# Last recurrence of a four-layer network: more routed tiles per state in the first two halves, ends of halves twice as fast, experts without delay, the gate in its half

## Chip, cores and metric

One core of a Trainium2 chip runs the whole network in one launch. The metric is the device time of one execution in microseconds (us). The engines run on their own lists of instructions, each in its order, and wait for each other by semaphores: PE (TensorE, matmul; PEld loads its weights), DVE (VectorE), ACT (ScalarE), POOL (GpSimd) and SP (SyncE, which issues most transfers; POOL issues gathers and accumulating transfers). PSUM is the memory that matmuls write, in eight banks.

## The reference, cut to what matters

A batch of 4 sequences of 1024 rows and 128 features goes through four layers, each an "attention" and a feed-forward part with a layer norm behind the sum. The change lies in the third layer's feed-forward part (routed experts) and the fourth layer, `x` being float32 throughout:

```python
def _L2_ffn_ref(x, router_w, w13, w2):       # 8 experts, the best two a row
    probs = jax.nn.softmax(jnp.einsum('bsh,eh->bse', x, router_w), axis=-1)
    weights, indices = jax.lax.top_k(probs, 2)
    ...

def _L3_attn_ref(resid, ...):                # E = 256 channels, N = 16 states
    x = resid * lax.rsqrt(jnp.mean(resid * resid, -1, keepdims=True) + EPS) * norm_w
    skip = x @ skip_w.T
    xe = x @ in_w.T
    ...                                      # causal convolution of 4, silu -> xs
    delta = jax.nn.softplus(xs @ wd1.T @ wd2.T + wd2_b)
    A = -jnp.exp(A_log)
    Bm = xs @ wb.T
    Cm = xs @ wc.T
    def step(h, inp):
        d_l, b_l, c_l, x_l = inp
        h = jnp.exp(d_l[:, :, None] * A) * h + (d_l * x_l)[:, :, None] * b_l[:, None, :]
        y_l = jnp.einsum('ben,bn->be', h, c_l)
        return (h, y_l)
    ...
    y = (y + xs * W_D) * jax.nn.silu(skip)
    return resid + y @ out_w.T

def _L3_ffn_ref(x, Wr, br, W1, b1, W2, b2):  # 8 experts, all computed, gated by top-p
    ...
    h = jax.nn.relu(jnp.einsum('bth,ehf->betf', x, W1) + b1[None, :, None, :])
    y = jnp.einsum('betf,efh->beth', h, W2) + b2[None, :, None, :]
    return jnp.einsum('bte,beth->bth', gate, y)
```

## The kernel before

The kernel is written with generators: a part of the work is a Python generator that issues instructions and yields, and a driver calls `next` on several of them by turns. A library puts the instructions of this stage into an order for each engine from what it reckons to be ready, so a list's order follows the driver's turns but isn't the same. Buffers come from pools that turn round in the order of issue; a tile waits until the one it takes the place of has been read.

The fourth layer works on eight halves of sequences (`halves` in `l3`, 512 rows each; half 0 and 1 are of the first sequence). For each half there are four pieces of work:

- `l3_prepare`: norm, convolution, `xs`; then `pdb` on PE (line 1784 copies it on ACT, line 1785 writes the rows `Bm` and `Cm` to DRAM, from where SP reads them back on all partitions as `bn` and `cn`), and `pd` on PE, from which ACT and DVE make `dl` (delta) and, in line 1809, `ud` (delta times `xs`).
- `l3_scan`: the recurrence, one state of 16 at a time for all 512 rows. POOL makes `db = ud * bn` (line 1845), ACT `da = exp(dl * A)` (1849), DVE scans (1850), POOL makes `hc = db * cn` (1861). From half 2 on (`b > 0`) POOL joins the `hc` of two states by an accumulating transfer (line 1865); PE sums `hc`, or the joined pairs, into two banks with an identity matrix (`pys`). Halves 0 and 1 thus have 16 sums and the others 8, the eighth with states 14 and 15.
- `l3_sum`: the last sums, and `xs * W_D + pys` on DVE (line 1882); `l3_finish`: the gate (`psk` on PE, tanh on ACT, two products on DVE), the output projection (`po`), the norm, and the router of the experts (`prl`, then a chain on DVE that ends with `gt`). Then the half goes to the list `todo`.
- `l3_experts`: the eight experts of each half in `todo`, one half after the other: `pgt` and `pb2` first, then for each expert four `ph` (128x512) with a ReLU on ACT (line 1973), sixteen `py` (128x128) and four accumulating steps on DVE (1989); weights `wh` are loaded by SP two experts ahead. On PE every float32 matmul shows as two records in the trace.

`moe` is the third layer's routed part, still running: per tile (23 a sequence, 92 in all) SP loads the expert's weights `wx`, PE does four `ph` and two `py`, and after a sequence's last tile POOL gathers 16 blocks of rows (line 1529) for its combination. Its tiles of the last sequence can't begin before that sequence's rows have been scattered, by `m2["rest"]`, one step a state.

The driver is the loop over `l3_scan(u)` in `l3`: after each state of half `i` it takes one step of the end of the half before (`end`, `l3_sum` and `l3_finish`), one of the next half's preparation (`nxt`), one of `moe` (two in half 0), and three of the experts, or four once `moe` has ended. A half in `todo` ages by one a state, and its experts start when it is older than 3. All of these matmuls but `pys` take their banks from four that go by the tag `ff`. What is left at a half's end of `end` and `nxt` is issued there, and before halves 1, 3 and 5 as much of `moe` as the half behind them needs.

Of the kernel before, what the change touches and what calls it, by code (L numbers as in the profile page):

```python
# [10 lines left out]
F32 = mybir.dt.float32  # L11
I32 = mybir.dt.int32
U32 = mybir.dt.uint32
AF = mybir.ActivationFunctionType
ALU = mybir.AluOpType
# [3 lines left out]
P = 128  # L19
# [21 lines left out]
E3, NST, DDELTA, KCONV = 256, 16, 64, 4  # L41
# [17 lines left out]
class Net:  # L59
# [1535 lines left out]
    def l3(self, moe, fp):  # L1595

        c3 = self.c3  # L1600
        halves = [dict(b=b, h=h) for b in range(B) for h in range(2)]
        for i, u in enumerate(halves):
            u["prev"] = halves[i - 1] if u["h"] else None
        halves[0] = dict(self.c3["first"], **{k: halves[0][k] for k in ("prev",)})
        for i, u in enumerate(halves[1:], 1):
            u["prev"] = halves[i - 1] if u["h"] else None
        work = self.l3_experts(fp)
        end = iter(())
        for i, u in enumerate(halves):
            nxt = iter(())  # L1610
            if i + 1 < len(halves):
                if halves[i + 1]["h"] == 0:
                    while "done" not in self.m2["st"][halves[i + 1]["b"]]:
                        next(moe)
                nxt = self.l3_prepare(halves[i + 1])
            for f in self.l3_scan(u):
                next(end, None)
                next(nxt, None)
                for k in range(1):
                    next(self.m2["rest"], None)  # L1620
                busy = next(moe, moe) is not moe
                if i == 0:
                    for k in range(1):
                        next(moe, None)
                for k in range(3 if busy else 4):
                    next(work)
                for v in c3["todo"]:
                    v["age"] += 1
            for f in chain(end, nxt):
                pass  # L1630
            end = chain(self.l3_sum(u), self.l3_finish(u))
        for f in end:
            next(work)
        c3["all"] = True
        for f in work:
            pass

    def l3_experts(self, fp):


        c3 = self.c3
        heads, self.wh = [], {}

        def others():

            while len(heads) < 2 and c3["todo"] and ("all" in c3 or c3["todo"][0]["age"] > 3):
                heads.append((c3["todo"].pop(0), []))
            return heads[1:]

        i = 0  # L1650
        while True:
            others()
            if "all" in c3 and c3["banks"]:

                c3["banks"].close()
                c3["banks"] = None
                c3["ctx"].enter_context(self.banks(ff=8))
            if heads:
                u = heads[0]
                if not u[1]:  # L1660
                    yield from self.l3_ffn_head(*u, fp)
                yield from self.l3_ffn(*u, i, fp, others)
                heads.pop(0)
                i += NE
            elif "all" in c3:
                return
            else:
                yield
# [146 lines left out]
    def l3_scan(self, u):  # L1815


        nc, c3, b, h = self.nc, self.c3, u["b"], u["h"]
        sp, wp, aneg = c3["sp"], c3["wp"], c3["aneg"]
        wout = c3["we"][:, :, ND:]  # L1820
        xnT, xs, dl, ud, rows = (u[k] for k in ("xnT", "xs", "dl", "ud", "rows"))
        carry = wp.tile([P, 2, NST], F32, name="carry") if h == 0 else u["prev"]["carry"]
        u["carry"] = carry
        u["py"] = py = []
        u["sums"] = sums = []

        def add(n, hc):
            if not py:
                py.extend(self.psb(f"y{ec}", [P, 512], f"pys{ec}") for ec in range(2))
                u["first"] = n  # L1830
            for ec in range(2):
                self.mm(py[ec], self.ident, hc[:, ec, :], n == u["first"], n == NST - 1)

        u["add"] = add
        for n in range(NST):
            bc = []
            for i, nm in enumerate(("bn", "cn")):
                t = wp.tile([P, 1, 512], F32, name=nm, bufs=4)
                r = i * NST + n
                nc.sync.dma_start(  # L1840
                    out=t[:, 0, :], in_=rows[r : r + 1, :].to_broadcast([P, 512])
                )
                bc.append(t.to_broadcast([P, 2, 512]))
            db = wp.tile([P, 2, 512], F32, name="db", bufs=4)
            nc.gpsimd.tensor_mul(db, ud, bc[0])  # L1845
            for ec in range(2):
                j = ec * NST + n
                da = self.psb("da", [P, 512], "da")
                nc.scalar.activation(da, dl[:, ec, :], AF.Exp, scale=aneg[:, j : j + 1])  # L1849
                nc.vector.tensor_tensor_scan(  # L1850
                    db[:, ec, :],
                    da,
                    db[:, ec, :],
                    carry[:, ec, n : n + 1] if h else 0.0,
                    ALU.mult,
                    ALU.add,
                )
            if h == 0:
                nc.scalar.copy(carry[:, :, n : n + 1], db[:, :, 511:512])
            hc = wp.tile([P, 2, 512], F32, name="hc", bufs=4)  # L1860
            nc.gpsimd.tensor_mul(hc, db, bc[1])  # L1861
            if n % 2 and b > 0:

                hc0 = sums.pop()[1]
                nc.gpsimd.dma_start(out=hc0, in_=hc, accum_op=ALU.add)
                sums.append((n, hc0, n + 2))
            else:
                sums.append((n, hc, n + 2))
            for k in range(2):
                if sums and sums[0][2] <= n:  # L1870
                    add(*sums.pop(0)[0:2])
            yield

    def l3_sum(self, u):

        while u["sums"]:
            u["add"](*u["sums"].pop(0)[0:2])
            if u["sums"]:
                yield
        for ec in range(2):  # L1880
            x = u["xs"][:, ec, :]
            self.nc.vector.scalar_tensor_tensor(
                x, x, self.col("W_D", i=ec), u["py"][ec], ALU.mult, ALU.add
            )

    def l3_finish(self, u):


        nc, c3, b, h = self.nc, self.c3, u["b"], u["h"]
        sp, wp = c3["sp"], c3["wp"]  # L1890
        ff = lambda s, n: self.psb("ff", s, n)
        wout = c3["we"][:, :, ND:]
        yt = u["xs"]
        for ec in range(2):
            p = ff([P, 512], "psk")
            self.mm(p, c3["wskip"][:, 0, ec * P : (ec + 1) * P], u["xnT"])

            t = sp.tile([P, 512], F32, name="th")
            nc.scalar.activation(t, p, AF.Tanh, scale=0.5)
            nc.vector.scalar_tensor_tensor(p, t, 1.0, p, ALU.add, ALU.mult)  # L1900
            nc.vector.scalar_tensor_tensor(
                yt[:, ec, :], yt[:, ec, :], 0.5, p, ALU.mult, ALU.mult
            )
            yield
        po = ff([P, 4, D], "po")
        for k in range(4):
            for ec in range(2):
                self.mm(
                    po[:, k, :],
                    yt[:, ec, k * P : (k + 1) * P],  # L1910
                    wout[:, ec, :],
                    ec == 0,
                    ec == 1,
                )

        r = sp.tile([P, 4, D], F32, name="ss_r", tag="s2")
        nc.vector.scalar_tensor_tensor(
            r, self.xN[b][:, 4 * h : 4 * h + 4, :], 2.0, po, ALU.mult, ALU.add
        )
        yield  # L1920
        yield from self.norm_parts(wp, r, b, 4 * h, 4, ps=ff, act=True, slow=True)
        yield
        n = NC // 2
        pr, g, rank, pj, cum = self.router(sp, b, c3["wr"], c3["br"], ps=ff, c0=4 * h, n=n)
        q, cum = cum
        nc.vector.tensor_mul(g, q, pj)
        nc.vector.reduce_sum(cum, g, AX.X)

        nc.vector.tensor_single_scalar(cum, cum, TOP_P, ALU.is_lt)
        nc.vector.scalar_tensor_tensor(cum, rank, 1.0, cum, ALU.is_le, ALU.max)  # L1930
        u["gt"] = sp.tile([P, n, NE], F32, name="gt", bufs=8)
        nc.vector.tensor_mul(u["gt"], pr, cum)
        u["age"] = 0
        c3["todo"].append(u)
# [268 lines left out]
```

## Time and profile before

| what | us |
| --- | --- |
| median of 3 runs (lowest, highest) | 2328.13 (2327.18, 2331.37) |
| profiled execution | 2329.42 |
| its span, first to last instruction | 2327.6 |
| PE busy in the span | 1994.8 (86%) |
| DVE | 1348.4 (58%) |
| ACT | 1205.4 (52%) |
| POOL | 1024.8 (44%) |

The span is what the views of the profile divide; 1.8 us of the profiled execution lie around it. Up to about 1400 us the first three layers run, and the eight halves of the recurrence lie between 1407 and 2177 us, by POOL's `hc` products; behind them come the experts that are left. A share of busy time over the whole span says little about either stage, so the stages have to be read one by one. In rows of the view of time, the columns are start, duration, engine, line, operation, out<-in, shape, count, and in brackets how long the engine had been idle and what ended that; a PE row's line is that of the helper that issues all matmuls (127), so that a tile's name tells which it is.

### The profile page before, as it was taken

The page shows a single profiled execution, that of the slowest core. Times are in us where ns is not written, and L with a number is a line of the kernel's source. Part 1 is how long each engine was busy: PE and PEld are TensorE (multiplying, and loading weights), DVE is VectorE, ACT ScalarE, POOL GpSimd, SP SyncE. Part 2 cuts the span into 40 slices and gives each one's busy share as a digit, 9 for nine tenths or more (in the row PEclk, how much of TensorE's full clock was granted, in tenths as well). Part 3 has the DMA queues.
Part 4 walks back from the last instruction along what each step waited for, and adds up shares of the span by engine and source line. Part 5 has one row for each costly group of instructions (what it writes and reads, how often), then busy time and mean ns, then how long its engine had stood idle before and what let it go on. Part 6 is the DMA issues. An engine that isn't in the chain of part 4 may idle for free. (4 is left out here: it accounts for less than half of the span.)

```text
span 2327.6 us, 46367 instructions
## 1 busy us (share of the span) xinstructions
PE 1994.8 (86%) x17802; PEld 1395.0 (60%) x17802; DVE 1348.4 (58%) x3693; ACT 1205.4 (52%) x2617; POOL 1024.8 (44%) x813
## 2 busy tenths in 40 slices
PE   6667979979999999999979857678898989889888
PEld 3455655544477777787767654355655556546556
DVE  7458743433445554654655557767776767776421
ACT  6543433332244444454565556566668766666343
POOL 5000230000123244234143259989887887769300
PEclk9757979979999999999999978889999989899899
DMA  3000110014000010031222176457765666666421
GB/s 105 0 19 18 31 38 6 14 40 140 1 3 2 3 37 22 25 88 42 84 77 72 49 221 182 146 165 204 219 175 162 180 173 163 180 164 177 100 59 50
DMA packets 138701, 211.62 MB, mean 91 GB/s; under 512 B 18613, under 2 KB 75952, under 8 KB 138096
## 3 DMA queue, kind: packets, MB, share of 16 engines
q1 hardware_dynamic: 126192, 173.87, 24.7%
q0 software_dynamic: 12288, 34.79, 7.2%
q8 instruction: 140, 2.29, 0.4%
q14 instruction: 81, 0.66, 0.1%
HBM read 160.29 MB, written 23.16 MB: 79 GB/s over the span
## 5 line engine op out<-in xcount | busy, mean ns | idle before, releaser
L1059 POOL TENSOR_TENSOR qt<-r_q,sb_c_turn 128x256 f32<-128x256 f32 (+1 forms) x256 | 164.4, 663 | 446.7 <-ACT r_q L1051 441.0
L1861 POOL TENSOR_TENSOR hc<-db,cn 128x1024 f32<-128x1024 f32 x128 | 311.3, 2453 | 64.4 <-PE pys L127 20.4
L1845 POOL TENSOR_TENSOR db<-ud,bn 128x1024 f32<-128x1024 f32 x112 | 283.7, 2597 | 30.6 <-DVE pmv L159 19.1
L127 PEld LDWEIGHTS py<-wh,hh 128*128 128x128 f32 x2048 | 251.8, 196 | 67.8 <-issue 38.7
L127 PE MATMUL ph<-xT,wh 128*128 128x512 f32 x512 | 262.5, 634 | 21.7 <-ACT hh L1973 8.0
L127 PE MATMUL py<-wh,hh 128*128 128x128 f32 x2048 | 257.2, 280 | 13.0 <-ACT hh L1973 10.1
L1973 ACT ACTIVATE hh<-ph,sb_cols 128x512 f32<-128x512 f32 x256 | 170.6, 682 | 146.2 <-PE ph L127 119.9
L1117 DVE TENSOR_TENSOR a<-pa_m,sb_c_near 128x256 f32<-128x256 f32 x256 | 96.6, 419 | 204.2 <-PE pa_m L127 204.2
L1074 ACT ACTIVATE kN<-kp_mo,sb_c_trig 128x128 f32<-128x128 f32 x448 | 130.2, 372 | 131.9 <-PE kp_mo L131 122.1
L1849 ACT ACTIVATE da<-dl,aneg 128x512 f32<-128x512 f32 x224 | 153.2, 689 | 84.1 <-DVE db L1850 83.3
L127 PE MATMUL pys<-hc,sb_c_ident 128*128 128x512 f32 x320 | 162.0, 636 | 24.6 <-POOL hc L1861 15.0
L1850 DVE TENSOR_TENSOR_SCAN db<-da,carry,db 128x512 f32<-128x512 f32 x128 | 156.8, 1266 | 25.9 <-ACT da L1849 12.5
L127 PEld LDWEIGHTS ph<-xT,wh 128*128 128x128 f32 x512 | 93.5, 202 | 115.0 <-issue 65.7
L1850 DVE TENSOR_TENSOR_SCAN db<-da,db 128x512 f32<-128x512 f32 x128 | 149.1, 1205 | 14.3 <-ACT da L1849 8.2
L1989 DVE SCALAR_TENSOR_TENSOR h_acc<-py,gt,h_acc 128x128 f32<-128x128 f32 x256 | 71.9, 342 | 140.4 <-PE py L127 140.4
L127 PE MATMUL pqk<-xT,wE 128*128 128x256 f32 x512 | 137.7, 393 | 8.2 <-ACT coT L1193 4.2
L127 PEld LDWEIGHTS pys<-hc,sb_c_ident 128*128 128x128 f32 x320 | 61.7, 206 | 90.0 <-issue 59.1
L127 PEld LDWEIGHTS pqk<-xT,wE 128*128 128x128 f32 x512 | 89.4, 195 | 22.1 <-DVE cv L1036 8.1
L729 POOL DMA_INDIRECT orows<-o,ix x20 | 18.9, 946 | 185.3 <-DVE o L727 158.8
L131 PE MATMUL pt<-sb_c_ident,xN 128*128 128x128 f32 x224 | 54.5, 345 | 52.1 <-ACT xN L174 33.9
L1193 ACT COPY coT<-pt 128x512 f32<-128x512 f32 x64 | 37.6, 587 | 114.7 <-PE pt L131 114.7
L127 PE MATMUL po<-ht,wD 128*128 128x512 f32 x192 | 93.7, 595 | 0.0
(457 smaller groups left out, 4342.4 us busy)
## 6 DMA issues: line engine op xcount, KB each, us to landing
wx<-in_wF SPq DMA_DIRECT2D x92, 384.0 KB, 3.4
bn<-rows SPq DMA_DIRECT2D x128, 256.0 KB, 4.9
cn<-rows SPq DMA_DIRECT2D x128, 256.0 KB, 4.5
wh<-in_wH SPq DMA_DIRECT2D x64, 512.0 KB, 3.9
hc<-hc POOLq DMA_DIRECT2D x48, 512.0 KB, 7.1
xrows<-zero SPq DMA_DIRECT2D x4, 1472.0 KB, 12.4
xg<-xrows SPq DMA_DIRECT2D x20, 256.0 KB, 3.1
yrows<-ys SPq DMA_DIRECT2D x20, 256.0 KB, 3.3
```

The lines of the kernel that those rows point to most:

```text
L127: return self.nc.tensor.matmul(out=out, lhsT=lhsT, rhs=rhs, start=start, stop=stop)
L131: self.nc.tensor.transpose(out, in_, self.ident[0:n, 0:n])
L1059: nc.gpsimd.tensor_mul(u["qt"][:, m, a:], u["q"][:, a:], c2["turn"][:, m, o + a : o + 2 * P])
L1074: self.nc.scalar.activation(u["kN"][:, c, m, :], pk[:, c, :], AF.Copy, scale=trig[:, k, m : m + 1])
L1117: nc.vector.tensor_mul(u["a"][:, i, :, :], pa[i], self.c2["near"][:, None, :].to_broadcast([P, 2, P]),)
L1193: nc.scalar.copy(oT, pt)
L1845: nc.gpsimd.tensor_mul(db, ud, bc[0])
L1849: nc.scalar.activation(da, dl[:, ec, :], AF.Exp, scale=aneg[:, j : j + 1])
L1850: nc.vector.tensor_tensor_scan(db[:, ec, :], da, db[:, ec, :], carry[:, ec, n : n + 1] if h else 0.0, ALU.mult, ALU.add,)
L1861: nc.gpsimd.tensor_mul(hc, db, bc[1])
L1973: nc.scalar.activation(ht, ph, AF.Relu, bias=self.col("h_b1", i=e * NK + k))
L1989: nc.vector.scalar_tensor_tensor(acc[:, c, :], py[:, c, :], gt[:, c, e : e + 1], acc[:, c, :], ALU.mult, ALU.add,)
```

## The change

It issues the same kinds of instructions in other turns:

- per state, `end` takes two steps and not one; `moe` takes four in half 0 (two before), two in half 1 (one before) and one in the others as before; the experts take three in the last half in any case;
- a half's experts may start once it is older than 0, not 3;
- the gate moves out of `l3_finish` (where it took two steps) into `l3_gate`, called inside `l3_scan` at states 9 and 12 of the same half, with a tile for each of the two channel blocks; `l3_sum` multiplies by it;
- in the last half the last two states aren't joined by a transfer, so that it has nine sums.

```diff
+            u["final"] = final = i + 1 == len(halves)
             for f in self.l3_scan(u):
-                next(end, None)
+                for k in range(2):
+                    next(end, None)
                 next(nxt, None)
...
                 busy = next(moe, moe) is not moe
-                if i == 0:
-                    for k in range(1):
-                        next(moe, None)
-                for k in range(3 if busy else 4):
+                for k in range((3, 1)[i] if i < 2 else 0):
+                    next(moe, None)
+                for k in range(3 if busy or final else 4):
                     next(work)
...
-            while len(heads) < 2 and c3["todo"] and ("all" in c3 or c3["todo"][0]["age"] > 3):
+            while len(heads) < 2 and c3["todo"] and ("all" in c3 or c3["todo"][0]["age"] > 0):
...
             nc.gpsimd.tensor_mul(hc, db, bc[1])
-            if n % 2 and b > 0:
-
+            if n in (9, 12):
+                self.l3_gate(u, n // 12)
+            if n % 2 and b > 0 and not (u["final"] and n == NST - 1):
                 hc0 = sums.pop()[1]
                 nc.gpsimd.dma_start(out=hc0, in_=hc, accum_op=ALU.add)
...
         for ec in range(2):
-            x = u["xs"][:, ec, :]
+            x, p = u["xs"][:, ec, :], u["py"][ec]
             self.nc.vector.scalar_tensor_tensor(
-                x, x, self.col("W_D", i=ec), u["py"][ec], ALU.mult, ALU.add
+                p, x, self.col("W_D", i=ec), p, ALU.mult, ALU.add
+            )
+            self.nc.vector.scalar_tensor_tensor(
+                x, u["gate"][ec], 0.5, p, ALU.mult, ALU.mult
             )
+
+    def l3_gate(self, u, ec):
+
+        nc, c3 = self.nc, self.c3
+        p = self.psb("ff", [P, 512], "psk")
+        self.mm(p, c3["wskip"][:, 0, ec * P : (ec + 1) * P], u["xnT"])
+        t = c3["sp"].tile([P, 512], F32, name=f"th{ec}")
+        nc.scalar.activation(t, p, AF.Tanh, scale=0.5)
+        nc.vector.scalar_tensor_tensor(t, t, 1.0, p, ALU.add, ALU.mult)
+        u.setdefault("gate", []).append(t)
...
-        for ec in range(2):
-            p = ff([P, 512], "psk")
-            self.mm(p, c3["wskip"][:, 0, ec * P : (ec + 1) * P], u["xnT"])
-
-            t = sp.tile([P, 512], F32, name="th")
-            nc.scalar.activation(t, p, AF.Tanh, scale=0.5)
-            nc.vector.scalar_tensor_tensor(p, t, 1.0, p, ALU.add, ALU.mult)
-            nc.vector.scalar_tensor_tensor(
-                yt[:, ec, :], yt[:, ec, :], 0.5, p, ALU.mult, ALU.mult
-            )
-            yield
```

## The prediction

> **What bounds the kernel now.** I read the page first, then busy time by stretches cut at the ends of the halves, then POOL's waits, then the order of time on PE, POOL and DVE at one change of halves. Below, each stretch but the first and the last runs from the end of a half's last `hc` product (state 15; I call that moment T) to the next half's T. Columns: us, then busy PE, PEld, DVE, ACT, POOL, the granted PE clock, DMA.
>
> ```profile
> 1407.10:1471.90 64.80, 46.58 (x139) 23.34 (x140) 42.07 (x60) 38.48 (x79) 64.80 (x29) 0.83 0.52 160
> 1471.90:1579.10 107.20, 80.10 (x364) 52.49 (x363) 78.42 (x140) 67.43 (x136) 91.81 (x50) 0.90 0.55 163
> 1579.10:1670.40 91.30, 76.48 (x394) 52.29 (x394) 71.85 (x139) 63.83 (x136) 79.82 (x39) 0.96 0.73 205
> 1670.40:1791.00 120.60, 105.86 (x535) 70.00 (x534) 85.26 (x164) 85.90 (x155) 100.52 (x59) 0.96 0.66 179
> 1791.00:1879.10 88.10, 79.79 (x357) 49.08 (x356) 67.46 (x136) 64.42 (x125) 75.72 (x38) 0.94 0.67 178
> 1879.10:1968.70 89.60, 85.46 (x424) 56.47 (x423) 62.80 (x108) 58.64 (x97) 81.47 (x42) 0.96 0.64 171
> 1968.70:2076.80 108.10, 97.20 (x465) 62.72 (x464) 76.44 (x151) 75.82 (x132) 81.97 (x42) 0.94 0.67 179
> 2076.80:2176.60 99.80, 84.27 (x402) 54.20 (x401) 68.23 (x136) 59.21 (x92) 81.31 (x41) 0.91 0.62 167
> 2176.60:2327.60 151.00, 134.13 (x703) 94.08 (x701) 34.24 (x120) 58.09 (x93) 0.88 (x1) 0.92 0.19 55
> ```
>
> Half 0 is POOL's alone (64.80 of 64.80). In halves 2 to 7 POOL has 76 to 82 us of work a half (100.5 with the 16 gathers of half 3) and PE nearly as much; the length of a half is POOL's work plus its waits. After the last T only PE works, on experts. POOL's waits from half 2 on (total, times, longest):
>
> ```profile
> POOL hc L1861 <- PE pys L127: 20.4, 11, 5.2
> POOL db L1845 <- DVE pmv L159: 19.1, 1, 19.1
> POOL db L1845 <- issue: 11.5, 1, 11.5
> POOL yg L1529 <- ACT xN L174: 7.6, 1, 7.6
> ```
>
> The second and third are single waits at changes of halves (5 to 6, 6 to 7): the next half's first `db` needs `ud`, the end of `l3_prepare`. At the other changes POOL goes on within 0.5 to 2.1 us. The change 6 to 7, POOL and PE in order of time (start, us):
>
> ```profile
> 2077.14 0.88 POOL L1865 DMA_DIRECT2D hc<-hc  x1 [0.30 <-DVE h_acc L1989]
> 2089.52 9.25 POOL L1845 TENSOR_TENSOR db<-ud,bn 128x1024 f32<-128x1024 f32 x4 [11.51 <-issue]
> ```
> ```profile
> 2070.73 1.96 PE L127 MATMUL pd<-db,sb_s_d 65*128 65x512 f32 x4
> 2072.53 3.74 PE L127 MATMUL py<-wh,hh 128*128 128x128 f32 x32
> 2076.11 3.60 PE L127 MATMUL pys<-hc,sb_c_ident 128*128 128x512 f32 x8
> 2085.92 3.78 PE L127 MATMUL pys<-hc,sb_c_ident 128*128 128x512 f32 x4 [6.21 <-DMA hc<-hc]
> ```
>
> What to see: PE goes through its list in its order. The half's last `pys` can't run before the accumulating DMA of the last pair has landed, 9.1 us after T (2076.81 to 2085.92), and all behind it waits. Here `pd` (what `ud` is made of) stands ahead of that `pys`; so `ud` lags only because DVE has L1882, which needs that `pys`, in front of the second `ud`.
>
> **The change, part by part.** I take the order in which the built programs' instructions stand on each engine, and price it with rows of before. H6.8 is the eighth (last) `pys` pair of half 6.
>
> *Ends twice as fast, experts at once.* In the changed order experts of half h-1 start at H.4 to H.6 of half h, before at H.7 or behind the half. Behind the last `pys` of all stand 224 `py` and 52 `ph` of experts, before 256 and 60: two experts fewer. One expert is 3.44 (`ph`) + 3.57 (`py`) us in the chain that ended last, so 14.0 us leave the tail. Price of the move: the experts' matmuls now stand in front of the next half's `pdb` and `pd`. In before, `pd` stands two or more pairs ahead of the last `pys` at every change (ahead of H6.6, H5.7, H4.5). In the changed order:
> - 5 to 6 and 6 to 7: H.8, 16 `py`, 2 `ph`, then `pd`. So T + 9.1 (DMA) + 2.1 (`pys`, 2085.92 to 2088.01) + 3.6 + 1.7 + 2.0 (`pd`) = T+18.5 for `pd`.
> - 4 to 5: `pd` is behind H4.7, `pdb` and an expert's 16 `py` and 2 `ph`. POOL issues that pair's DMA two `hc` (2.45 each) and 0.9 before T; it lands at T+3.0; + 2.1 + 1.9 + 5.3 + 2.0 = T+14.3.
> - 3 to 4: second `pd` behind H3.6, 13 `py`; its DMA is issued at T-11.8 (three `hc`, a `db`, two issues), lands T-3.0; + 2.1 + 1.0 + 2.9 + 1.0 = T+4.0.
> - 2 to 3: H2.8, then 16 `py`, a `ph`, `pdb`, 3 `ph` (these hide ACT's 0.7 for L1784), `pd`: T + 9.1 + 2.1 + 4.4 + 1.9 + 2.6 + 2.0 = T+22.1.
>
> From `pd` to the second `ud`: 13.3, 16.3, 14.4, 14.1, 16.0, 13.5 us in before, and 11.7 (2072.7 to 2084.4) had L1882 not stood between. While POOL stalls, ACT and DVE have no scans, so I take 12; ends 11.7 and 16.3. First `db`: T+30.5 twice, T+26.3, T+16, T+34.1. Before: T+20.8, +12.7, +0.6, +2.1, +0.5. Differences 9.7, 17.8, 25.7, 13.9, 33.6. In the last, 8 of the 16 gathers (L1529, 1.25 us apart) now lie in the stall, 10 us, and the 7.6 us wait ahead of them goes: 16.0 left. Sum **+83**. Behind the waiting H.8 on PE are the experts and `pd`; on DVE the new L1884, and behind it `h_acc` and `dl`; on POOL `db`, thus the whole next half. The 87 us from a half's first `db` to its T (1989.5 to 2076.8, 2089.5 to 2176.6) remain. PE can't refill POOL's lost time: its work between two last `pys` is 75 to 100 us, less than the periods of 103 to 118 us that result.
>
> In exchange PE comes to each half less late. Of the in-half waits of POOL, 20.4 (`pys`), 3.0 (`hc` DMA) could go, 23 us at most, 0 at least; I take half, **-12**.
>
> *Last half:* the last pair isn't joined by a DMA: one `pys` pair (1.7 us) more on PE, one issue (0.9) less on POOL, and no 9.1 us after T. But the pair before, issued 3.4 us before T, still stands ahead: it lands at T+5.4, and + 2.1 + 0.9 + 3.4 puts the last `pys` at T+11.8 (before T+14.2). Then the changed order has no expert between the router's `prl` and `pgt`, which took 10.6 us in half 7 of before (2165.6 to 2176.2): about 10 us of idle PE. Tail: 2.4 earlier, 14.0 of experts and 0.9 of a `psk` already done, less 10 for the router: **-7** (bounds 0, if the psk left over holds `po` up as well, and -17, if the router is covered after all).
>
> *Tiles of the routed pair, four and two a state:* **0**. Half 0 is POOL's, and its PE list even shrinks (2 tiles of two `py` there, 5 before; 19 in half 1, 15 before): the tiles run out until the last batch's rows are scattered. Cover: POOL's 92 us and 15 of waits in half 1; PE's work there grows by 5 to about 85 of 107. If SP's `wx` issues, now ahead of several `bn`, hold these back (POOL waited 4.9 us for `bn` once), +8.
>
> *Gate at states 9 and 12:* **0**. Same two matmuls, tanh and products; for halves 2 to 6 both `psk` still stand behind the last `pys` in PE's list, so it isn't in its own half. ACT has four table loads fewer (1.28 each), in an engine 57 to 65% busy.
>
> Sum: 83 - 12 - 7 = +64 on a span of 2327.6, so 2391.6; around the span the profiled execution has 1.8 us more (2329.4), the median of the three is 2328.1, so on the median I say **2391**.
>
> Two rules of the Trainium skill differ from rows here. "DMA: Bandwidth & Descriptors" (Anatomy of one DMA, SWDGE path) fits a transfer as 2.0 us plus bytes over 436 GB/s: an estimate of 3.2 us for the 512 KB of `hc`, where the rows show 7.1 median and 8.8 at this place; the sum by the rule would be about 20 us lower, near 2371. "TensorE: Matmul & The Clock Gate" (Part 1: the HAM clock gate) has PE at half rate after idling until some 3.4 us of work: agrees with the last row above (3.78 us where 1.88 is usual), and would add up to 3.4 us at each of five changes, up to 2408.
>
> **The rivals.**
> 1. *PE is the bound, and the stalls cost nothing* (faster). For it: PE 86% busy, tail PE alone. Then only the tail counts: 2328 - 7 = 2321; with the two waits of 19.1 and 11.5 gone too, 2290. Against: in the stretches of those two waits PE idled 11 and 15 us, so it wasn't the bound there. Decides: `pd` reached before T at changes 4 to 7. Chance 0.12.
> 2. *Same mechanism, half the price* (slower): all 23 us of in-half waits go, `pd` to `ud` takes 11, the DMA its median 7.1 (-1.7 at four changes): 2391 - 11 - 5 - 7 = 2368; with the tail at -17, 2358. Chance 0.18.
> 3. *SP's queue starves POOL in halves 0 and 1 on top* (slower): SP spent 10.74 us on two `wx` at 1377.90; one or two such stretches ahead of `bn`, 2391 + 16 = 2407. Against: only 4.9 us of such a wait in before. Chance 0.12.
> 4. *No net change*, stalls and tail cancelling: 0.03.
>
> **How the numbers follow.** My forecast gets 0.55, its own range 2368 to 2415 (`pd` to `ud` at 16.3 is +21 over the five changes, all in-half waits left +12). With 2 and 3, slower has 0.85. A measurement of this kernel tells 0.2% (4.7 us) from no change; that leaves 0.03 for same and 0.12 for faster. Range 2340 to 2416: it reaches below rival 2 and leaves out rival 1 and the case of both upper bounds at once.
>
> **What would show it.** Right: POOL idle 25 to 34 us before the first `db` of halves 3, 5, 6 and 7, released by DVE `ud`; periods near 115 us for halves 5 to 7; tail near 144 us; half 0 unchanged. Wrong: `db` of these halves within 15 us of T; or a half's 87 us shrinking below 80, since PE and DVE would then have set it.

## The result and the profile after

| | before | after |
| --- | --- | --- |
| median (lowest to highest), four runs each | 2327.65 (2323.45 to 2331.37) | 2421.97 (2416.41 to 2426.76) |
| span of the profiled execution | 2327.6 | 2422.6 |
| PE busy | 1994.8 (x17802) | 2026.7 (x17806) |
| POOL busy | 1024.8 | 1022.2 |

The changed kernel takes 1.0386 times as long (95% interval 1.0359 to 1.0414): 94 us more where +64 was forecast. The instructions are all but the same: POOL, which sets the length of the halves, has the same work and waits more, and PE's matmuls took 32 us longer for the same work.

In the changed kernel's numbering `db` is L1846, the scan L1851, `hc` L1862, `ud` L1810, `dl` L1811, the router's `gt` L1936 and the ReLU `hh` L1977. First the busy time by stretches, cut as before: half 0 from its first `hc`, then from T to T, then the tail (us, PE, PEld, DVE, ACT, POOL, granted PE clock, DMA share, GB/s).

```profile
1410.60:1481.40 70.80, 46.94 (x102) 19.83 (x102) 45.82 (x62) 41.50 (x82) 67.36 (x30) 0.79 0.42 124
1481.40:1581.00 99.60, 81.08 (x417) 56.15 (x418) 74.48 (x139) 63.50 (x133) 87.09 (x47) 0.95 0.64 189
1581.00:1691.60 110.60, 96.16 (x511) 67.23 (x511) 74.49 (x154) 67.80 (x141) 88.55 (x48) 0.95 0.68 186
1691.60:1828.10 136.50, 114.41 (x492) 70.15 (x491) 84.65 (x172) 91.91 (x164) 89.12 (x49) 0.88 0.52 138
1828.10:1934.50 106.40, 83.91 (x380) 54.00 (x379) 70.94 (x130) 62.79 (x116) 81.08 (x41) 0.89 0.59 155
1934.50:2049.20 114.70, 92.06 (x403) 57.35 (x402) 71.90 (x131) 64.95 (x103) 81.06 (x40) 0.87 0.57 148
2049.20:2167.00 117.80, 90.66 (x408) 57.30 (x407) 72.10 (x133) 68.53 (x128) 81.00 (x40) 0.88 0.56 146
2167.00:2287.70 120.70, 98.91 (x445) 62.18 (x444) 67.69 (x123) 63.33 (x98) 81.07 (x41) 0.87 0.55 147
2287.70:2422.60 134.90, 115.75 (x634) 82.12 (x632) 32.41 (x115) 48.11 (x78) 0.00 (x0) 0.94 0.18 51
```

Halves 2 to 7 are 106 to 137 us long where they were 88 to 121; POOL's work from the T of half 1 to that of half 7 is the same (501.9 us, before 500.8), so the growth is POOL's waits. The tail is 134.9, it was 151.0. Half 0, which was to stay unchanged, took 70.8 us and not 64.8. The granted clock has dropped to 0.87 to 0.89 in halves 3 to 7; it was 0.91 to 0.96.

POOL's waits in the recurrence of the changed kernel (total, times, longest):

```profile
POOL db L1846 <- DVE ud L1810: 57.6, 4, 27.6
POOL db L1846 <- ACT dl L1811: 50.3, 2, 27.1
POOL hc L1862 <- PE pys L127: 36.4, 11, 7.1
POOL hc L1862 <- DVE db L1851: 20.9, 11, 4.8
POOL yg L1529 <- ACT xN L174: 16.7, 1, 16.7
```

The first two are the waits at the changes of halves that the forecast was about (the `dl` of ACT belongs to the same end of `l3_prepare`). The third was 20.4 before; the forecast had it shrink.

Where in a half this comes from is seen on PE. Rows around the change 6 to 7 (T = 2167.0), some left out:

```profile
2130.86 0.48 PE L131 MATMUL pt<-sb_c_ident,xN 128*128 128x128 f32 x1 [7.24 <-ACT xN L174]
...
2152.18 1.01 PE L131 MATMUL pgt<-sb_c_ident,gt 128*8 128x128 f32 x4 [7.14 <-DVE gt L1936]
...
2155.85 3.78 PE L127 MATMUL ph<-xT,wh 128*128 128x512 f32 x4
...
2162.72 1.88 PE L127 MATMUL pys<-hc,sb_c_ident 128*128 128x512 f32 x4
...
2171.45 1.88 PE L127 MATMUL pys<-hc,sb_c_ident 128*128 128x512 f32 x4
...
2174.88 1.88 PE L127 MATMUL pys<-hc,sb_c_ident 128*128 128x512 f32 x4
...
2178.13 3.06 PE L127 MATMUL py<-wh,hh 128*128 128x128 f32 x26
...
2181.89 1.88 PE L127 MATMUL pd<-db,sb_s_d 65*128 65x512 f32 x4
```

And POOL at the same change:

```profile
2164.69 2.35 POOL L1862 TENSOR_TENSOR hc<-db,cn 128x1024 f32<-128x1024 f32 x1 [7.12 <-PE pys L127]
...
2195.34 6.99 POOL L1846 TENSOR_TENSOR db<-ud,bn 128x1024 f32<-128x1024 f32 x3 [27.12 <-ACT dl L1811]
```

Read from the top: PE stands still for 7.24 us before the norm's `pt` and for 7.14 us before `pgt`, in the router's chain of the half before. Only then do that half's experts begin, at 2155.85, 11 us before T. So they stand before the last three of this half's eight sums (the `pys` of 2162.72 is the sixth, and POOL's `hc` of state 15 waits 7.12 us for it) and before the next half's `pd` (2181.89, over at T+16.8; forecast T+18.5). The eighth sum, at 2174.88, has no bracket, so it waited for nothing: the transfer of its pair had landed 5.4 us behind T (5.8 at the change 5 to 6, where that sum didn't wait either), and PE was busy with experts beyond that. `ud` starts at 2193.9, the first `db` at T+28.3 (forecast T+30.5).

That PE now lacks experts in the middle of a half, and has them in a bunch at its end, is in the rows of all later halves. From the last `py` of one half's experts to the first of the next half's there were 13, 6, 13, 19, 26 and 21 us in before (halves 0 to 6); in the changed kernel there are 19, 19, 41, 42, 45 and 40. And where in before the first `py` of a half's experts came 8 to 32 us behind the next half's T, from half 2 on it now comes 3 to 16 us ahead of it. In the hole PE has sums, the next half's preparation and the router's chain, and waits for this chain:

```profile
PE pgt L131 <- DVE gt L1936: 37.6, 6, 8.1
PE pt L131 <- ACT xN L174: 21.6, 4, 7.2
```

In before the waits ahead of `pgt` were 11.0 us, those ahead of `pt` nothing. The end of a half isn't earlier for its two steps a state: its `po` starts 50 to 65 us behind T in halves 2 to 6 (24 to 61 in before), as the experts stand in front of it.

The account, in the forecast's own terms (POOL's idle time from the T of half 1 to the T of half 7, by what came behind it; us):

| term | forecast | measured |
| --- | --- | --- |
| waits before `db` at the changes, with those of the gathers | +83 | +77.3 and +8.8 = +86.1 |
| POOL's waits inside the halves (`hc`) | -12 (0 to -23) | +20.7 (53.5 to 74.2) |
| tail | -7 (0 to -17) | -16.2 |
| halves 0 and 1 (tiles, gate) | 0 | +9.5 - 7.6 = +1.9 |
| POOL's work and its own issues | 0 | +2.3 |
| sum | +64 | +94.8 |

### The profile page after: what moved, and what is told of

The parts are those of the page before. It is cut to its first block, busy times and chain, and to the rows that moved or that the text cites. A ratio compares the mean times of both kernels' runs of the same rounds, so it can differ in the third digit from the quotient of the medians.

```text
span 2422.6 us, 46380 instructions
## 1 busy us (share of the span) xinstructions
PE 2026.7 (84%) x17806; PEld 1409.8 (58%) x17806; DVE 1353.4 (56%) x3693; ACT 1202.1 (50%) x2613; POOL 1022.2 (42%) x812
## 4 chain that ended last, share of the span: by engine, by line
PE 40%; DVE 14%; ACT 8%; issue 5%; DMA 4%; POOL 3%; SPq 0%; ACTq 0%; POOLq 0%; DVEq 0%
PE ph L127 6%; PE py L127 6%; DVE db L1851 5%; PE po L1126 5%; PE pqk L127 4%; PE pa_m L127 4%; PE pys L127 2%; PE kp_mo L127 2%; PE pv L127 2%; PE pr L1196 2%; POOL db L1846 1%; PE pt L131 1%; POOL hc L1862 1%; DMA hc<-hc 1%; PE kp_mo L131 1%
## 5 line engine op out<-in xcount | busy, mean ns | idle before, releaser
L1862 POOL TENSOR_TENSOR hc<-db,cn 128x1024 f32<-128x1024 f32 x128 | 316.9, 2532 | 85.7 <-PE pys L127 36.4
L1846 POOL TENSOR_TENSOR db<-ud,bn 128x1024 f32<-128x1024 f32 x112 | 291.0, 2650 | 107.9 <-DVE ud L1810 57.6
L127 PE MATMUL ph<-xT,wh 128*128 128x512 f32 x512 | 267.7, 641 | 22.3 <-ACT hh L1977 6.2
L1977 ACT ACTIVATE hh<-ph,sb_cols 128x512 f32<-128x512 f32 x256 | 171.0, 681 | 152.6 <-PE ph L127 126.0
L127 PE MATMUL pys<-hc,sb_c_ident 128*128 128x512 f32 x324 | 175.3, 670 | 37.6 <-POOL hc L1862 19.5
L1074 ACT ACTIVATE kN<-kp_mo,sb_c_trig 128x128 f32<-128x128 f32 x448 | 129.8, 371 | 131.9 <-PE kp_mo L131 121.9
L1851 DVE TENSOR_TENSOR_SCAN db<-da,carry,db 128x512 f32<-128x512 f32 x128 | 156.5, 1265 | 23.4 <-POOL db L1846 16.8
L1851 DVE TENSOR_TENSOR_SCAN db<-da,db 128x512 f32<-128x512 f32 x128 | 149.7, 1207 | 19.2 <-POOL db L1846 17.8
```

The source lines that it names most:

```text
L127: return self.nc.tensor.matmul(out=out, lhsT=lhsT, rhs=rhs, start=start, stop=stop)
L1074: self.nc.scalar.activation(u["kN"][:, c, m, :], pk[:, c, :], AF.Copy, scale=trig[:, k, m : m + 1])
L1851: nc.vector.tensor_tensor_scan(db[:, ec, :], da, db[:, ec, :], carry[:, ec, n : n + 1] if h else 0.0, ALU.mult, ALU.add,)
L1977: nc.scalar.activation(ht, ph, AF.Relu, bias=self.col("h_b1", i=e * NK + k))
```

## The experiments

Each is compared with the kernel before on the same chip. Four chips were used, one for each four runs; before takes 2331.6 us on the first and 2367 to 2370 on the others, where all comes later from the start of the recurrence on (the first half's T at 1500 to 1516 us, on the first chip at 1474 to 1482). So beside the ratio stands R, the time from the T of half 0 to the end of the span, which is 855.8 in before and 941.2 in after by the traces above. R is from one profiled execution, and for one kernel on two chips it differed by up to 10 us (5 and 14, after and 13, 7 and 10), so that smaller differences between chips say nothing. "As 7" and "gate in its half" in the table include one more line of the change: in the last half the experts take three steps a state and not four.

| experiment | median | ratio (95% interval) | R |
| --- | --- | --- | --- |
| 1 after, one step of the end | 2351.7 | 1.0080 (1.0051 to 1.0109) | 865.7 |
| 2 after, experts older than 3 | 2348.1 | 1.0069 (1.0052 to 1.0086) | 868.7 |
| 3 before, two steps of the end, experts at once | 2375.4 | 1.0186 (1.0168 to 1.0204) | 899.2 |
| 4 before, tiles four and two | 2341.3 | 1.0039 (1.0022 to 1.0056) | 861.8 |
| 5 after, last sums behind `pd` and `ud` | 2436.0 | 1.0280 (1.0254 to 1.0306) | 930.3 |
| 6 after, experts three steps throughout | 2387.3 | 1.0090 (1.0058 to 1.0122) | 876.4 |
| 7 before, gate in its half, nine sums | 2338.0 | 0.9866 (0.9839 to 0.9893) | 828.7 |
| 8 before, last sums behind `pd` and `ud`, nine sums | 2357.6 | 0.9938 (0.9912 to 0.9964) | 840.3 |
| 9 as 7, last sums behind `pd` and `ud` | 2337.9 | 0.9874 (0.9835 to 0.9913) | 825.9 |
| 10 as 7, again | 2339.5 | 0.9889 (0.9852 to 0.9927) | 829.3 |
| 11 as 7, tiles four and two | 2342.3 | 0.9903 (0.9873 to 0.9933) | 825.9 |
| 12 after, tiles as before | 2422.5 | 1.0228 (1.0195 to 1.0261) | 917.7 |
| 13 after, again | 2449.9 | 1.0331 (1.0304 to 1.0359) | 946.8 |
| 14 as 5, again | 2432.1 | 1.0281 (1.0241 to 1.0320) | 920.6 |
| 15 5 and 6 together | 2366.3 | 0.9994 (0.9974 to 1.0013) | 855.6 |
| 16 before, gate in its half | 2330.2 | 0.9843 (0.9820 to 0.9867) | 822.8 |

### 1 to 4: the parts

1 and 2 undo one line each of the changed kernel; 3 and 4 put two, or one, into the kernel before:

```diff
 # 1, in after
-                for k in range(2):
-                    next(end, None)
+                next(end, None)
 # 2, in after
-  ... c3["todo"][0]["age"] > 0):
+  ... c3["todo"][0]["age"] > 3):
 # 3, in before: both of these the other way round
 # 4, in before
-                if i == 0:
-                    for k in range(1):
-                        next(moe, None)
+                for k in range((3, 1)[i] if i < 2 else 0):
+                    next(moe, None)
```

> The changed kernel with one step of `end` a state again. Theory (place of the next half's `pd` in PE's list): in this list `pd` stands ahead of or just behind H.7 at every change of halves (behind H2.5, H3.6, H4.6, H5.7, H6.6), so POOL's first `db` should come about 1, 13, 13, 21 and 13 us behind T, 61 us together where the changed kernel has 137 and before has 37. That is about 2345 us (2330 to 2365). Rival A (the routed tiles and their gathers, crowded into halves 1 and 2, and the clock that falls behind them): they are kept, so 2400 or more. Rival B (the gate in its own half and the nine sums): kept too, 2400 or more.

> The changed kernel with experts starting only when a half is older than 3 again; ends keep two steps. Theory: `pd` stands behind H2.7, H3.5, H4.8, H5.7 and H6.6, which gives first `db` at about 21, 6, 26, 22 and 16 us behind T, 91 together: about 2372 us (2350 to 2395). PE's waits for `pgt` (37.6 us in the changed kernel) should fall by half or more. Rivals A and B: 2400 or more.

> Before with these two parts alone: two steps of `end` a state, experts at age 1; no other part. Theory: `pd` behind H2.6 (12 us of experts further), H3.6 (12), H4.6 (8), H5.8 (7) and H6.8 (2): first `db` at about 24, 24, 20, 29 and 26 us behind T, 123 together: about 2400 us (2375 to 2420). Rivals A and B: within 15 us of before, 2313 to 2343, since their parts are absent.

> Before with the routed tiles' pace alone (four a state in half 0, two in half 1). Theory: `pd` stays ahead of the last `pys` at every change (behind H2.4, H3.4, H4.7, H5.6, H6.6): first `db` about 5, 3, 23, 15 and 13 us behind T: 2340 us (2325 to 2355). Rival A: most of the loss is here, 2380 or more. Rival B: within 10 us of before.

Undoing either the fast end or the early experts takes nearly the whole loss away: POOL's `db` waits fall from 107.9 to 63.8 and 67.2 us, PE's wait for `pgt` from 37.6 to 22.5 and 14.6. The rivals that put the loss elsewhere than on end and experts are out by 1. But my numbers for 2 and 3 were 24 and 25 us too high: I had added up parts that don't add. With gate and tiles in place (R = 825.9, experiment 11) the fast end alone adds 42.8 us (2), the early experts alone 39.8 (1), and both together 115.3 (after). Without the other parts the same two together add only 43.4 us to before (3), and with gate and nine sums but not the tiles 89.0 (12 against 7); why they cost more beside the other parts is open. Tiles alone cost 0.4%.

### 5, 6 and 13 to 15: what stands in front of `pd`

The forecast had two things in front of `pd`: the last `pys`, which wait for a DMA, and the experts. 5 takes the first away, 6 thins out the second; 13 to 15 are after, 5, and both edits at once, on one chip.

```diff
 # 5, in after: on PE the sums of the last two pairs behind the next half's pd,
 # on DVE (in the same way) the sum with xs behind its ud
+            v = u.get("next", {}).get("pd_at") if n >= NST - 3 else None
+            with self.tc.issue_after(v) if v is not None else nullcontext():
                 for ec in range(2):
                     self.mm(py[ec], self.ident, hc[:, ec, :], n == u["first"], n == NST - 1)
...
 # 6, in after
-                for k in range(3 if busy or final else 4):
+                for k in range(3):
```

> The changed kernel, with the last two `pys` pairs of a half put behind the next half's `pd` on PE, and the products of l3_sum behind its `ud` on DVE. Theory as in the prediction (`pd` is late because it stands behind sums that wait for a DMA): POOL's wait before the first `db` falls by about 9 us at the changes after halves 2, 4, 5 and 6: 2385 us (2375 to 2395). Rival C (the experts, bunched in the second part of the half, are what stands in front; PE is busy anyway while the DMA flies): only the 2.1 us of each pair and PE's short waits for the DMA go, 2 to 4 us a change: 2405 to 2418.

> The changed kernel with three steps of the experts a state throughout (four once the routed tiles had ended, in the changed kernel). In PE's list `pd` then stands behind H4.5, H5.6 and H6.6 and not H4.7, H5.8 and H6.8; as much expert work as in the changed kernel is left behind the last sum (52 `ph`, 224 `py`). Rival C (bunched experts): PE's waits for `pgt` and `pt` (59 us in the changed kernel) fall below 40, POOL's wait for `db` (108 us from half 2 on) to about 60, time 2375 us (2355 to 2390). If bunching isn't it and PE's total work is: no gain, 2412 or more.

> The changed kernel itself, beside its variants on one chip, since the earlier variants ran on other chips than it did and the time ahead of the first half's T differs there. Every theory: time from that T to the end of the span near 941 us (935 to 948). If the part ahead of T is to blame for the earlier differences, the ratio comes out at 1.030 to 1.036 on a chip where the kernel before takes some 2368 us.

> The changed kernel with the last two pys pairs behind the next half's pd and the sum with xs behind its ud, as in the earlier run of that name. Theory (experts bunched by the idle router's chain hold pd, the sums only POOL's hc): 5 to 18 us shorter than the changed kernel on this chip. Rival (the joining DMA in front of pd is a good part of the waits): 30 us shorter or more.

> The changed kernel with both: experts three steps a state throughout, and the last sums behind pd and ud. Theory (once the experts are spread, the sums are what is left in front of pd, as in the kernel before): 10 to 25 us shorter than with the spread alone, time from the first half's T to the end 850 to 868 us, waits before db 25 to 40 us. Rival (the spread experts are still in front): 872 us or more, db waits 45 us or more.

POOL's waits in 13 and in 14, then PE's for the router in 6:

```profile
POOL db L1846 <- DVE ud L1810: 59.8, 4, 28.2
POOL db L1846 <- ACT dl L1811: 50.3, 2, 27.1
```
```profile
POOL db L1851 <- DVE ud L1813: 53.8, 4, 28.9
POOL db L1851 <- ACT dl L1814: 48.8, 2, 26.2
```
```profile
PE pgt L131 <- DVE gt L1936: 18.1, 6, 5.3
```

5's ratio alone could be read either way (times the 2328 of the result above it is 2393, near the theory with the DMA), as it ran on another chip than after; that is why 13 and 14 were run side by side. 13 came out as expected (ratio 1.0331, R 946.8). In 14 the last two pairs' sums stand behind `pd`, and yet the waits before `db` are 102.6 us against 110.2; `pd` ends 8 to 19 us behind T at the changes from 3 to 4 on (2 to 17 in 13). So the DMA of the last pair, from which the forecast counted its T + 9.1, didn't set the time of `pd`, as the rows of after at 2174.88 already say: the experts behind `pgt` are late enough by themselves. 14 is 17.8 us faster than 13 by the medians (R by 26 in the two profiles), and its profile shows POOL's `hc` waits as the place (53.2 against 75.7 us).

In 6 the same experts are spread by three steps a state. The holes between the experts of two halves shrink to 10 to 20 us, `pgt` of halves 3 to 6 starts 71 to 79 us behind T (after: 90 to 103), the waits before `db` fall to 49.3 us and R to 876.4: 65 of the 85 us that were lost, more than the 47 expected. The change 2 to 3, where the gathers lie, stays as bad (first `db` at T+36.9); its cause is left open. 15 brings R to 855.6, level with before, as expected; but not by `db`, whose waits stay at 52.0 us (25 to 40 expected): `hc` falls again, from 68.0 to 47.1. So the order of the sums counts mainly for POOL's waits inside the halves; why it does wasn't traced further.

### 7, 8, 10 and 16: parts put into the kernel before

7 is the kernel before with the gate at states 9 and 12 of its own half and the nine sums of the last half, the two parts that the forecast had at nothing in the recurrence; 10 repeats it, and 16 has the gate without the nine sums. All three, and 9 and 11 below, also keep the three steps of the experts in the last half, though the texts of what was expected call the parts alone. 8 is before with 5's order of sums, and nine sums.

> Before with the gate in its own half and the nine sums of the last half alone. Theory (place of `pd`): behind H2.4, H3.5, H4.5, H5.8 and H6.5, so that only the change after half 5 gets later (about +7 us) and the tail shorter (about 5): 2330 us (2322 to 2338). Rival B (the gate itself costs, by its banks or by tanh on ACT): 2345 or more.

> Before with L1882 of l3_sum put behind the next half's `ud` on DVE, the last two pairs behind `pd` on PE, and nine sums in the last half. Theory: at the change after half 6 `ud` came 5.0 us late only because of L1882 (2084.4, not 2089.4), after half 5 some 1.5; the tail a little shorter: 2320 us (2312 to 2328), a version that beats both. If L1882 isn't what held `ud`: 2328 as before.

> The same kernel as the earlier run of gate and nine sums, to compare it with its neighbours on one chip. Theory: ratio 0.9866 (0.983 to 0.990) whatever the chip. Rival (the gain belonged to that chip): 0.995 or above.

> The kernel before with the gate at states 9 and 12 of its own half and nothing else: the last half keeps its eight sums. Theory (the gate is most of the gain of the pair, since the tail's nine sums save a few us at most): ratio 0.990 (0.986 to 0.994). Rival (the gain is the nine sums' in the last half): 0.996 or above.

16 has the lowest ratio of all kernels, 1.6% under before, and 7 and 10 are little behind it, so the nine sums add nothing that shows. 7 and 16 gained more than was expected. But how much of it is the gate's is open, since the kernel before with the three steps in the last half and nothing else wasn't run. Of the 33.0 us of R between before (in the first trace) and 16, 27.3 lie where that line acts, in the last half and the tail (250.8 us, then 223.5), and 5.7, less than chips can differ by, in halves 1 to 6 (605.0, then 599.3).

With `psk`, tanh and two products out of the half's end, `po` starts 32, 22, 50, 47, 38 and 20 us behind T in halves 2 to 7 of experiment 16, where in before it was 46, 24, 52, 61, 50 and 30, and PE waits 0.3 us for `pgt` (11.0). The tail is 135.0 us (151.1) with nearly the same work left in it (512 records of `py` in both, 122 of `ph` against 128): PE is busy for 121.9 us of it at a clock of 0.97, in before 134.1 at 0.92. One large wait is left at a change of halves, at 5 to 6:

```profile
POOL db L1846 <- DVE ud L1810: 24.3, 1, 24.3
```

8 shows that the forecast's view of the change 6 to 7 of *before* was right: with the sum with `xs` behind `ud`, the first `db` comes at T+2.0 and not T+12.7 (the last two sums, which 8 puts behind `pd`, already stood behind it there).

### 9, 11 and 12: together, and the tiles

9 joins 7 and 8; 11 is 7 with the tiles' pace, that is the changed kernel with its end and ages set back; 12 is the changed kernel with the tiles' pace set back.

> The kernel before with the gate at states 9 and 12, nine sums in the last half (both as in the earlier run of that pair, ratio 0.9866), and besides the last two pys pairs of a half behind the next half's pd on PE, and the sum with xs behind the next half's ud on DVE. Theory (the first db of the next half is held by pd and ud, and with slow ends and late experts nothing else stands in front of pd): the 24 us wait before the first db at the change 5 to 6 goes, about 33 us of db waits become some 15, ratio 0.980 (0.975 to 0.986). Rival (the late sums delay the end of the half and the experts behind it, so that the time comes back as experts behind the last half): 0.9866 or above.

> The changed kernel with one step of the end a state and experts older than 3, as in the kernel before; what is left of the change is the gate, the nine sums and the tiles' pace. Theory (ends and ages do all of the harm, and tiles cost their 0.4 per cent whatever stands beside them): ratio 0.9905 (0.985 to 0.996), T of the first half's end to the end of the span near 840 us. Rival (the early tiles leave PE without work in later halves, and cost more once the gate is out of the ends): 1.000 or above.

> The changed kernel with the tiles' pace as before (two steps a state in the first half, one afterwards). Theory (two end steps and experts at once do the harm together, by idle PE before pgt and experts bunched behind it): ratio 1.034 (1.025 to 1.041), PE's waits before pgt and pt still above 40 us in sum. Rival (the tiles that are gone by half 4 are what PE lacks in the middle of the later halves): 1.020 or below, pgt and pt waits below 30 us.

9 adds nothing to 7, as its rival had it: the 24.3 us wait at 5 to 6 is still 20.6. 11 is faster than before. Its half 6, in the columns of the stretches above, and PE at its end:

```profile
2021.50:2109.20 87.70, 81.91 (x403) 52.58 (x402) 67.63 (x128) 59.51 (x108) 81.16 (x41) 1.00 0.67 180
```
```profile
2103.82 1.88 PE L127 MATMUL pd<-db,sb_s_d 65*128 65x512 f32 x4
...
2107.76 0.60 PE L131 MATMUL pgt<-sb_c_ident,gt 128*8 128x128 f32 x4
```

Against the same half of the changed kernel (117.8 us, clock 0.88): `pd` starts 5.4 us before T = 2109.2 and not 14.9 us behind it; `pgt` finds `gt` ready (its row has no bracket), since experts filled the time of the router's chain; and PE has the full clock.

12 came out a little under its range in the ratio, and its waits before `pgt` and `pt` (41.4 us in sum) and `db` (104.2) are nearly those of after, so the rival, that early tiles leave PE without work, is out. Its R is 23.5 us shorter than that of after (29.1 than 13's), and this lies in half 1: 77.2 us long, 99.6 with the early tiles; POOL's own work is 12.9 us of that, gathers which 12 does in later halves. From there to the last T it takes 705.6 us, after 706.7, though 12 does the tiles and 16 gathers in that time on top: in sum they cost nothing in those halves, which have holes on PE, and in half 1 they do.

## Why the forecast missed

- **Direction and place** held. The changes' first `db` came at T+39.9, +16.4, +24.4, +28.8 and +28.3 where +34.1, +16, +26.3, +30.5 and +30.5 were forecast, and the term of +83 measured +86.1. Halves 5 to 7 were to be near 115 us and took 115 to 121. That the experts in front of `pd` do it is shown by 1, 2 and 6. The run from a half's first `db` to its T, taken as 87 us, was 89 to 92 from half 4 on. Two of the forecast's "first `db`" of before (+2.1 at 3 to 4, +0.5 at 2 to 3) are where POOL goes on behind T; the first `db` itself lies 13.2 and 8.8 us ahead of T there. Counted as idle time of POOL, the sum stands. "Half 0 unchanged" didn't hold (70.8 us for 64.8).
- **What failed is the term of -12** ("PE comes to each half less late"). Its bounds were a relief of 0 to 23 us, with no case of a loss. Added up by state over halves 2 to 7, POOL's `hc` waits in states 0 to 12 did fall, from 34.8 to 28.5 us; those in states 13 to 15 rose from 18.7 to 45.7. The relief was there at half its size, and at the end of the half a loss stood against it: 26.1 of the 45.7 us were ended by `pys` (6.3 before) and 13.2 by DVE's scan (1.4). The rows above show the place, sums behind the experts which the forecast had put in front of `pd` alone; that the order of the sums governs these waits is shown by 14 (21.0 us in states 13 to 15, 44.7 in 13), but 6, with the experts spread, leaves them at 41.0, and why the scans come later is open. The miss on the span is 95 - 64 = 31 us; this term alone is 33, and the others cancel (+3, +2, +2, -9).
- **Right in number by luck, wrong in reason**: at 5 to 6 and 6 to 7 the forecast had `pd` wait for the DMA of the last pair (T + 9.1). It landed at T+5.8 and T+5.4, and the last sum began at T+7.6 and T+7.8 without a wait, behind experts. 14 took that sum out of the way and the waits stayed.
- **PE idle in mid-half** was counted nowhere in the halves, only in the tail (10 us from `prl` to `pgt`). In the halves PE waited 59.2 us for `pt` and `pgt`. In the tail the wait was 6.4 us, three short ones of before (4.5 us) were gone, and the last sums ended at T+10.1 (forecast T+11.8), so that the tail came out at -16.2, near its lower bound of -17.
- **Gate "0"** isn't confirmed: put into before together with the three steps in the last half it is worth 1.6% (16), in favour of the change, but no run tells the two apart. The forecast looked at the order of `psk` against `pys`, and not at the chain from the half's sums to `po`, which lost two steps.
- **Tiles "0 (+8)"**: 0.4% alone (9 us), about its upper bound. With the rest they cost 23.5 us of R, in half 1 (after against 12). Rival 3 (SP's queue) isn't the reason there: POOL waits 0.9 us for a `wx` load in that half.
- Rival 1 (PE is the bound) fell by PE's waits, 130 us from the T of half 1 to that of half 7, before 68. Rival 2 (half the price) erred on the other side. With the measured +21 in the place of -12, the forecast's sum would have been 2424.

The Trainium skill's page "DMA: Bandwidth & Descriptors" (Anatomy of one DMA, SWDGE path) gave an estimate of 3.2 us for the joining transfer; its median was 5.6 us in the changed kernel and 7.1 in before, so the rows decide.

## What to carry to other kernels

When work that fills an engine's gaps is let start earlier, look for the place where it runs out: a backlog that looks like delay may be the cover of a latency (here the router's chain), and what used to be spread comes back as a bunch in front of whatever the next stage waits for. Price a moved block at every consumer behind it on the list, and give a hoped-for relief a bound on the other side of zero. Parts of a change of order don't add up, so try each part alone: two that cost 43 and 40 us cost 115 together, and they hid others (the gate, with three steps of the experts in the last half) that without them make the kernel 1.6% faster.

## What wasn't expected of the hardware

PE paid for the waits a second time, by its clock. Three stretches of the changed kernel around the `pgt` wait shown above (columns as before; the number behind POOL's is the granted clock):

```profile
2144.00:2156.00 12.00, 4.19 (x16) 2.49 (x14) 10.14 (x18) 5.31 (x11) 11.90 (x7) 0.63 0.31 67
2156.00:2160.00 4.00, 4.00 (x5) 1.70 (x6) 2.90 (x3) 1.02 (x2) 1.57 (x2) 0.50 0.51 98
2160.00:2172.00 12.00, 12.00 (x52) 7.26 (x51) 5.00 (x10) 4.83 (x9) 3.22 (x2) 0.96 0.34 59
```

PE is busy for all of the 4 us behind the wait, at half the clock, and the four `ph` of 2155.85 take 3.78 us where 1.88 is usual; behind them the clock is back at 0.96. That agrees with the page "TensorE: Matmul & The Clock Gate" (Part 1) of the Trainium skill, which has PE at half rate after an idle time until it has been busy for some 3.4 us, and from which the forecast had an estimate of up to 3.4 us at each of five changes; here it happens inside the halves. From half 0's T to the end the mean clock was 0.936 in before, 0.903 in after and 0.968 in experiment 16, and PE's busy time over the span rose by 31.9 us for four instructions more. How much of that reached the end of the span wasn't told apart from the waits.

The chips differ by up to 1.8% for the kernel before, and the changed kernel's ratio was 1.0386 on one and 1.0331 (13) on another; no run here shows why.
